# Two layers of graph attention: sending the rows of neighbour maxima of the one-head attentions by way of DRAM

## The chip, the cores and the metric

The kernel runs on one core of a Trainium2 chip. The metric is device time in microseconds (us), from the first to the last instruction of the program on that core. TensorE (PE), VectorE (DVE), ScalarE (ACT), GpSimd (POOL) and SyncE (SP, which here only issues transfers) each run their own queue of instructions in order, and wait for each other by semaphores.

## The reference

There are 32 graphs of 512 nodes with 512 features each, and an adjacency matrix for each graph. All values are float32. Two layers follow each other, each with a layer norm and a ReLU ahead and a residual added behind:

```python
# layer 0: one head
h = jnp.maximum(_layernorm(x), 0.0)
scores = leaky_relu(s_src[:, :, None] + s_dst[:, None, :] + attn_b[0], 0.2)
scores = jnp.where(adj + eye == 0, -inf, scores)
x = x + einsum('bij,bjh->bih', softmax(scores, axis=-1), h)
# layer 1: a four-head attention, then a one-head attention
h = jnp.maximum(_layernorm(x), 0.0)
h = elu(gat_layer(h, mask, W1, att_src1, att_dst1, b1, concat=True))   # 4 heads of 256
x = x + gat_layer(h, mask, W2, att_src2, att_dst2, b2, concat=False)   # 1 head of 512
```

Inside `gat_layer` the nodes are projected (`xl = x @ W`), each node gets two scores from `xl`, the score of an edge is `leaky_relu(asrc + adst)`, edges that are not there are masked, a softmax runs over the neighbours, and the weighted rows of `xl` are summed. So each graph has six attentions: one of layer 0, four heads, and one more of the second layer. In the kernel the first and the last of these are the one-head attentions, called layer 0 and layer 2; the heads are called layer 1.

## The kernel before

A graph's 512 nodes are T = 4 tiles of 128 partitions. Every attention goes through `edge_weights` (L582), which fills a buffer `E` of 128 x 4 x 512 with the unnormalised softmax weights, and through aggregation on PE (L627), which multiplies these weights with the values. The two projections are products of seven half-size blocks (`products`, L822).

`edge_weights` needs three rows that are the same in all 128 partitions: `a_row` (one score of all 512 nodes), `c_row` (the other score) and `m_row` (the greatest score over the neighbours of each node, which keeps the exponent in range). The work for one attention is:

- Row `a` is put in a PSUM bank. DVE takes, for each tile, the maximum of row and mask over the neighbours (L591), and two small operations (L596, L598) make of it the column `m` (128 x 4: the maximum of each node).
- Column `m` is made into a row: for each tile, PE transposes the column broadcast over 128 columns (`spread`, which calls `pe_transpose`, L487). Its result stays in the bank `m_bank`.
- For each of the four tiles: ACT computes the leaky ReLU of row `c` plus a column (L609), DVE subtracts the row `m` (L612), POOL adds the mask (L614), ACT takes the exponent (L617).

Rows `a` and `c` go another way for all but two attentions (layer 0 of graph 0 and layer 2 of graph 31, which use `spread`): `in_lines` (L547) transposes the columns of all scores at once (L553), an engine evicts the result, one transfer writes it to DRAM as lines of 512 values (L559), and `row_of` (L564) reads a line back with the same values for every partition (L569). For row `a`, ACT copies the row into a bank (`in_bank`, L576).

The places: `E` has 3, `E_one` (the weights of a one-head attention) has 2, `a_row` and `c_row` have one each, and the eight PSUM banks are six `acc`, one `a_bank` and one `m_bank`. The accumulators of projections and aggregations, and the transposes that precede an eviction, use `acc`.

The order of the work is written by a planner (`Plan`) while the program is built. Each operation is entered with an engine or a choice of engines, a modelled cost, and the buffers that it reads and writes. `draft` runs a list schedule over all operations: an engine takes the most urgent operation whose inputs are done and whose new buffers find a vacant place; buffers whose kind is listed as `in_turn` take their places in the order of entry. `latest` works out from a draft by when each operation must be done; six drafts are made, and the one that ends first is emitted. `AHEAD` makes an operation more urgent in the first draft. The modelled time from issue to landing is 3.0 us for lines and 4.5 us for a row.

Operations are entered graph by graph: projection of layer 1, aggregation of layer 2 of the graph before, the four heads, aggregation of layer 0 of the next graph (`layer0_out`), the scores of layer 0 of the graph after that (`layer0_scores`), projection of layer 2 and its edge weights (`layer2_project`). The planner moves them from there.

Of the kernel before, what the change touches and what calls it, by code (L numbers as in the profile page):

```python
# [15 lines left out]
P = 128  # L16
# [244 lines left out]
def kernel(  # L261
# [24 lines left out]
    nc = tc.nc  # L286
    B, N, D = x.shape
    H, F = att_src1.shape
    HF = H * F
    T = N // P  # L290
# [10 lines left out]
    psum = ctx.enter_context(tc.tile_pool(name="psum", bufs=1, space=PSUM))  # L301
# [11 lines left out]
    def places(kind, n, shape, dtype=F32, pool=big):  # L313
        return [pool.tile(shape, dtype, tag=f"{kind}{k}", name=f"{kind}{k}") for k in range(n)]
# [14 lines left out]
        "v": places("v", 2, [P, T, F]),  # L329
        "e": places("e", 1, [P, T // 2, F]),  # L330
        "col": places("col", 12, [P, T]),
        "ac": places("ac", 5, [P, 4, T]),
        "a_row": places("a_row", 1, [P, N]),
        "c_row": places("c_row", 1, [P, N]),
        "r": places("r", 8, [P, 1]),
        "st": places("st", 1, [P, T, nc.vector.BN_STATS_DIM]),
        "mv": places("mv", 1, [P, T, nc.vector.BN_AGGR_DIM]),
        "acc": places("acc", 6, [P, 512], pool=psum),
        "a_bank": places("a_bank", 1, [P, 512], pool=psum),
        "m_bank": places("m_bank", 1, [P, 512], pool=psum),  # L340
    }
    junk = big.tile([P, 512], BF16, name="junk")
    spill = ctx.enter_context(tc.tile_pool(name="spill", bufs=1, space=bass.MemoryType.DRAM))
    slots["spill"] = places("spill", 2, [N, D], pool=spill)
    slots["lines"] = places("lines", 8, [4, N], pool=spill)
    plan = Plan(slots, ("x", "spill", "m0", "m0T", "m1", "m1T", "h", "hT", "pair", "xl2", "E", "E_one", "v", "a_row", "c_row", "a_bank"))
    op = plan.op


    ident = const.tile([P, P], F32, name="ident")  # L350
# [30 lines left out]


    AHEAD, LATER = 400, 300


    QUARTER = (("11", "T1"), ("21", "22"))
# [142 lines left out]

        op(("ACT", "DVE"), (on_act(n, bias is not None), on_dve(n)), (by_act, by_dve), src, dst)  # L530

    def spread(kind, part, col_of, ahead):

        row = Buffer(kind)
        for t in range(T):
            pe_transpose(
                ahead, row, lambda t=t: row.at[:, node_block(t)], part, lambda t=t: col_of(t).to_broadcast([P, P]), ident, t
            )
        return row
# [4 lines left out]
        evict(values, ac(0), cols_of, place_of, 4 * T)  # L544
        return ac

    def in_lines(ac, part, n):  # L547

        pt, flat_, lines = Buffer("acc"), Buffer("e"), Buffer("lines")
        m = n * T  # L550
        op(
            "PE", on_pe(P, transpose=True),
            lambda: nc.tensor.transpose(pt.at[:m, :P], ac.at[:, :n, :].rearrange("p n t -> p (n t)"), ident),  # L553
            part + flat_("place"), pt(0), AHEAD,
        )
        evict(pt(0), flat_(0), lambda: pt.at[:m, :P], lambda: flat_.at[:m, 0, :P], P)
        op(
            "SP", by_dma(4 * m * P, 3000.0),
            lambda: nc.sync.dma_start(lines.at[:n].rearrange("n (t p) -> (n t) p", p=P), flat_.at[:m, 0, :P]),  # L559
            flat_(0), lines(0), AHEAD,  # L560
        )
        return lines

    def row_of(kind, lines, k):  # L564

        row = Buffer(kind)
        op(
            "SP", by_dma(4 * P * N, 4500.0),
            lambda: nc.sync.dma_start(  # L569
                row.at, bass.AP(tensor=lines.at.tensor, offset=lines.at.offset + k * N, ap=[[0, P], [1, N]])  # L570
            ),
            lines(0), row(*ROW), AHEAD,
        )
        return row

    def in_bank(kind, row):  # L576

        bank = Buffer(kind)
        op("ACT", on_act(N), lambda: nc.scalar.copy(bank.at, row.at), row(*ROW), bank(*ROW), AHEAD)
        return bank  # L580

    def edge_weights(kind, scores, ac, lines, k, mask_max, mask):  # L582


        a_of = lambda t: ac.at[:, k, t : t + 1]
        a_row = spread("a_bank", scores, a_of, AHEAD) if lines is None else in_bank("a_bank", row_of("a_row", lines, k))
        amax, z, m = Buffer("col"), Buffer("col"), Buffer("col")
        for t in range(T):
            op(
                "DVE", on_dve(N + 60),  # L590
                lambda t=t: nc.vector.tensor_tensor_reduce(  # L591
                    junk, mask_max.at[:, t, :], a_row.at, 1.0, LOWEST, ALU.add, ALU.max, accum_out=amax.at[:, t : t + 1]
                ),
                a_row(*ROW) + mask_max(*ROW), amax(t),
            )
        op("DVE", on_dve(T), lambda: nc.vector.tensor_add(z.at, ac.at[:, k + 1, :], amax.at), scores + amax(*ROW), z(0))  # L596
        op(
            "DVE", on_dve(T), lambda: nc.vector.scalar_tensor_tensor(m.at, z.at, SLOPE, z.at, op0=ALU.mult, op1=ALU.max),  # L598
            z(0), m(0),
        )  # L600

        E = Buffer(kind)
        m_row = spread("m_bank", m(0) + E("place"), lambda t: m.at[:, t : t + 1], AHEAD)
        c_of = lambda t: ac.at[:, k + 1, t : t + 1]
        c_row = spread("acc", scores + E("place"), c_of, AHEAD) if lines is None else row_of("c_row", lines, k + 1)
        for t in range(T):
            op(
                "ACT", on_act(N, 1),
                lambda t=t: nc.scalar.activation(E.at[:, t, :], c_row.at, AF.Prelu, bias=a_of(t), scale=1.0, alpha=SLOPE),  # L609
                c_row(*ROW) + scores, E(t),  # L610
            )
            op("DVE", on_dve(N), lambda t=t: nc.vector.tensor_sub(E.at[:, t, :], E.at[:, t, :], m_row.at), m_row(*ROW) + E(t), E(t))  # L612
            op(
                "POOL", on_pool(N, True), lambda t=t: nc.gpsimd.tensor_add(E.at[:, t, :], E.at[:, t, :], mask.at[:, t, :]),  # L614
                E(t) + mask(*ROW), E(t), lock=True,
            )
            op("ACT", on_act(N), lambda t=t: nc.scalar.activation(E.at[:, t, :], E.at[:, t, :], AF.Exp), E(t), E(t))  # L617
        return E
# [32 lines left out]
    X, S, M, L0, HT, L1, AC, H1T, L2 = {}, {}, {}, {}, {}, {}, {}, {}, {}  # L651
# [56 lines left out]
    def layer0_scores(b):  # L708
        rstd, nmr = layernorm(X[b])
        h0, ac = Buffer("h"), Buffer("ac")  # L710
        for t in range(T):
            relu_normed(h0, X[b], t, rstd, nmr)
            for i, w in ((1, ws_r), (0, wd_r)):
                op(
                    "DVE", on_dve(D), lambda t=t, w=w, i=i: dot(h0.at[:, t, :D], w, ac.at[:, i, t : t + 1]),
                    h0(t) + W["w0"](0, 1), ac((i, t)), lock=True,
                )
        c = ac(*((1, t) for t in ROW))
        op(
            "DVE", on_dve(T), lambda: nc.vector.tensor_scalar(ac.at[:, 1, :], ac.at[:, 1, :], b0_r, None, op0=ALU.add),  # L720
            c + W["w0"](2), c,
        )
        m0, m0T = masks0(b)
        scores = c + ac(*((0, t) for t in ROW))

        L0[b] = (h0, edge_weights("E_one", scores, ac, in_lines(ac, scores, 2) if b else None, 0, m0, m0T))

    def layer0_out(b):
        h0, E = L0.pop(b)
# [141 lines left out]
    def layer1_scores(b, h):  # L871
        xl, j = L1[b][h // 2], h % 2
        m1, m1T = M[b]
        if j == 0:
            ac = gather(
                xl(*((i, t) for t in range(T) for i in range(2))),
                lambda: xl_of(xl)[:, :, :, :2].rearrange("p t j i -> p j i t"), lambda: ac.at.rearrange("p (j i) t -> p j i t", j=2),
            )
            AC[b] = (ac, in_lines(ac, ac(0), 4))
        ac, lines = AC[b]  # L880
        return edge_weights("E", ac(0), ac, lines, 2 * j, m1T, m1)

    def layer1_head(b, h, E):

# [41 lines left out]
    def layer2_project(b):  # L926
        h1T = H1T.pop(b)
        L1.pop(b)
        m1, m1T = M.pop(b)

        xl = Buffer("xl2" if b < B - 1 else "pair")
        if b == B - 1:
            op("POOL", (110.0, 120.0), lambda: nc.gpsimd.memset(xl2_of(xl)[:, :, 2 + D :], 1.0), (), xl(2))

        def dst(i, j, r, c):
            t = i * (T // 2) + r
            return xl((j, t)), lambda: xl2_of(xl)[:, t, j * W2 : (j + 1) * W2]

        products(
            lambda i, j: h1T_of(h1T[j])[:, :, i * HN : (i + 1) * HN],  # L940
            lambda i, j, g: h1T[j](*((2 * g + k, i) for k in range(2))),
            PER, weights_of("w2", KINDS_2), W2, range(1), lambda w, k, c: w2_s[w][:, k, :], dst, [xl],
        )
        ac = gather(
            xl(*((0, t) for t in range(T))), lambda: xl2_of(xl)[:, :, :2].rearrange("p t i -> p i t"), lambda: ac.at[:, :2, :]
        )
        L2[b] = (edge_weights("E_one", ac(0), ac, in_lines(ac, ac(0), 2) if b < B - 1 else None, 0, m1T, m1), xl)

    def xl2_of(buf):
        return buf.at if buf.kind == "xl2" else buf.at[:, : T * (2 + D + 1)].rearrange("p (t f) -> p t f", t=T)  # L950
# [82 lines left out]
```

## Time and profile before

| | before |
|---|---|
| time | 3692.82 us, median of 3 runs (3692.64 to 3694.01) |
| profiled span | 3692.5 us |
| PE, weight loads (PEld), DVE, ACT, POOL busy | 98%, 85%, 78%, 48%, 43% |
| mean granted TensorE clock | 0.996 |
| matmuls on `m_bank` (L487) | 768, 117.1 us busy |
| line transposes (L553) | 126 (64 of 16 columns, 62 of 8) |
| copies of row `a` to its bank (L579) | 190, 582 ns each |
| rows read from DRAM | 190 of `a`, 190 of `c`, 256 KB each |

Busy times of PE overlap, since matmuls are pipelined: the time that an instruction costs is read from the distance between starts. In the timeline, a line merges instructions of one kind that follow each other; brackets at its end give the engine's idle time before it, and what ended it.

### The profile page before, as it was taken

To read this page: it belongs to the slowest core of one execution; us is meant where nothing else is said; L and a number is where in the kernel's file an instruction comes from. 1 tells how busy PE (TensorE), PEld (TensorE's weight loads), DVE (VectorE), ACT (ScalarE), POOL (GpSimd) and SP (SyncE) were. 2 spreads that over 40 slices of the span, in tenths; PEclk is the share of its full clock that TensorE was granted. 3 is DMA by queue.
4 is the path that set the end of the run, shared out by engine and by line. 5 is a ranking of instruction groups with operands and counts; after the bars stand their busy time and mean duration, and the time that the engine had idled before them with its cause. 6 is when DMAs were issued, how large, how long until landed. Compare 5 with 4: busy or idle time off the path is not lost.

```text
span 3692.5 us, 51317 instructions
## 1 busy us (share of the span) xinstructions
PE 3625.2 (98%) x17806; PEld 3131.3 (85%) x17806; DVE 2878.2 (78%) x7478; ACT 1760.2 (48%) x3227; POOL 1592.1 (43%) x1353
## 2 busy tenths in 40 slices
PE   5899999999999999999999999999999999999998
PEld 4788888888888888888888888888888888888887
DVE  7988778877788877788877878777887778787755
ACT  2455444554454554445544445544455544455433
POOL 3534444534444444445344444444444444444332
PEclk9999999999999999999999999999999999999999
DMA  6244322334323333223333233442233422334310
GB/s 162 52 92 103 87 73 82 81 92 104 72 74 90 75 103 91 70 83 80 91 103 72 76 88 75 103 98 68 81 82 85 103 72 78 86 75 103 90 51 32
DMA packets 304342, 312.17 MB, mean 85 GB/s; under 512 B 150496, under 2 KB 188880, under 8 KB 304080
## 3 DMA queue, kind: packets, MB, share of 16 engines
q1 hardware_dynamic: 270288, 275.32, 26.2%
q0 software_dynamic: 33792, 33.56, 6.5%
q8 instruction: 140, 2.29, 0.3%
q14 instruction: 122, 1.00, 0.1%
HBM read 240.91 MB, written 67.89 MB: 84 GB/s over the span
## 4 chain that ended last, share of the span: by engine, by line
PE 94%; DVE 3%; DMA 1%; POOL 0%; issue 0%; ACT 0%; DVEq 0%; ACTq 0%
PE acc L627 46%; PE acc L822 41%; PE acc L487 4%; PE m_bank L487 2%; DVE junk L591 1%; DVE junk L378 0%; PE acc L553 0%; DVE E L612 0%; DMA m<-in_adj_dram 0%; DVE v L905 0%; POOL E_one L614 0%; DVE E_one L612 0%; DMA x<-in_x_dram 0%; DVE v L893 0%; DMA out_dram<-x 0%
## 5 line engine op out<-in xcount | busy, mean ns | idle before, releaser
L614 POOL TENSOR_TENSOR E<-E,m 128x512 f32<-128x512 f32 x512 | 620.2, 1240 | 803.3 <-DVE E L612 798.3
L627 PE MATMUL acc<-pair,E 128*128 128x257 f32 x4096 | 961.6, 381 | 1.4 <-ACT E L617 1.2
L627 PEld LDWEIGHTS acc<-pair,E 128*128 128x128 f32 x4096 | 743.0, 190 | 114.5 <-ACT E L617 14.4
L822 PE MATMUL acc<-w_T,E 128*128 128x257 f32 (+1 forms) x2048 | 521.5, 381 | 1.0 <-ACT pair L522 0.6
L627 PE MATMUL acc<-h,E_one 128*128 128x256 f32 (+1 forms) x2048 | 478.2, 382 | 6.3 <-ACT E_one L617 6.3
L617 ACT ACTIVATE E<-E 128x512 f32<-128x512 f32 x512 | 312.0, 624 | 315.4 <-POOL E L614 315.4
L627 PE MATMUL acc<-xl,E_one 128*128 128x257 f32 x1984 | 448.2, 379 | 0.0
L591 DVE CUSTOM_DVE_ANT_0 junk<-m1T,a_bank 128x512 bf16<-128x512 bf16 x640 | 436.0, 681 | 15.4 <-PE a_bank L487 1.7
L627 PEld LDWEIGHTS acc<-h,E_one 128*128 128x128 f32 x2048 | 383.8, 191 | 59.4 <-ACT E_one L617 7.6
L822 PEld LDWEIGHTS acc<-w_T,E 128*128 128x128 f32 x2048 | 379.6, 190 | 55.4 <-ACT pair L522 0.8
L627 PEld LDWEIGHTS acc<-xl,E_one 128*128 128x128 f32 x1984 | 371.4, 190 | 53.7
L612 DVE TENSOR_TENSOR E<-E,m_bank 128x512 f32<-128x512 f32 x512 | 326.5, 679 | 24.7 <-PE m_bank L487 24.7
L609 ACT ACTIVATE E<-c_row,ac 128x512 f32<-128x512 f32 x512 | 335.6, 708 | 1.9 <-DMA c_row<-lines 1.9
L520 ACT COPY pair<-acc 128x258 f32<-128x258 f32 (+1 forms) x375 | 138.2, 369 | 412.1 <-PE acc L822 410.3
L520 ACT COPY xl<-acc 128x257 f32<-128x257 f32 x219 | 81.7, 373 | 455.8 <-PE acc L822 455.8
L902 ACT ACTIVATE e<-v,minus_one 128x512 f32<-128x512 f32 x256 | 184.3, 720 | 236.4 <-DVE r L639 111.1
L645 DVE SCALAR_TENSOR_TENSOR x<-acc,r,x 128x256 f32<-128x256 f32 x512 | 240.6, 478 | 47.8 <-PE acc L627 43.6
L663 POOL DMA_DIRECT2D m<-in_adj_dram x64 | 51.4, 804 | 521.1 <-DVE col L591 476.8
L835 DVE TENSOR_TENSOR pair<-acc,pair 128x258 f32<-128x258 f32 (+1 forms) x390 | 164.5, 424 | 137.8 <-PE acc L822 127.7
L822 PE MATMUL acc<-w,hT 128*128 128x258 f32 x1024 | 268.4, 382 | 0.0
L822 PE MATMUL acc<-w,pair 128*128 128x257 f32 x1024 | 259.3, 380 | 0.0
L614 POOL TENSOR_TENSOR E_one<-E_one,m 128x512 f32<-128x512 f32 x128 | 145.0, 1165 | 263.2 <-DVE E_one L612 263.2
(108 smaller groups left out, 6117.7 us busy)
## 6 DMA issues: line engine op xcount, KB each, us to landing
a_row<-lines SPq DMA_DIRECT2D x190, 256.0 KB, 3.4
c_row<-lines SPq DMA_DIRECT2D x190, 256.0 KB, 3.5
x<-in_x_dram SPq DMA_DIRECT2D x32, 1024.0 KB
m<-in_adj_dram POOLq DMA_DIRECT2D x64, 512.0 KB, 7.0
spill<-x SPq DMA_DIRECT2D x32, 1024.0 KB, 4.3
x<-spill SPq DMA_DIRECT2D x32, 1024.0 KB
out_dram<-x SPq DMA_DIRECT2D x30, 1024.0 KB, 5.0
m0T<-m SPq DMA_TRANSPOSE x128, 4.2
```

The source lines that it names most:

```text
L487: op("PE", on_pe(P, transpose=True), lambda: nc.tensor.transpose(dst_of(), src_of(), identity), src, dst(part), ahead)
L520: nc.scalar.copy(dst_of(), src_of())
L591: lambda t=t: nc.vector.tensor_tensor_reduce(junk, mask_max.at[:, t, :], a_row.at, 1.0, LOWEST, ALU.add, ALU.max, accum_out=amax.at[:, t : ...
L609: lambda t=t: nc.scalar.activation(E.at[:, t, :], c_row.at, AF.Prelu, bias=a_of(t), scale=1.0, alpha=SLOPE),
L612: op("DVE", on_dve(N), lambda t=t: nc.vector.tensor_sub(E.at[:, t, :], E.at[:, t, :], m_row.at), m_row(*ROW) + E(t), E(t))
L614: "POOL", on_pool(N, True), lambda t=t: nc.gpsimd.tensor_add(E.at[:, t, :], E.at[:, t, :], mask.at[:, t, :]),
L617: op("ACT", on_act(N), lambda t=t: nc.scalar.activation(E.at[:, t, :], E.at[:, t, :], AF.Exp), E(t), E(t))
L627: lambda s=s: nc.tensor.matmul(acc.at[:, :n], E.at[:, s, node_block(t)], of(s), start=(s == 0), stop=(s == T - 1)),
L645: lambda acc=acc, r=r, f=f, t=t: nc.vector.scalar_tensor_tensor(X.at[:, t, f], acc.at[:, :HD], r.at, X.at[:, t, f], op0=ALU.mult, op1=ALU. ...
L822: lambda k=k: nc.tensor.matmul(acc.at[:, :width], at[a]()[:, k, node_block(r)], weight_of(w, k, c), start=(first and k == 0), stop=(k == n ...
L835: op("DVE", on_dve(width), lambda: nc.vector.tensor_add(place(), acc.at[:, :width], place()), acc(0) + token, token)
L902: op("ACT", on_act(2 * F, 1), lambda e=e, ts=ts: nc.scalar.activation(e.at, v.at[:, ts, :], AF.Exp, bias=minus_one), parts, e(0))
```

## The change

Row `m` of most one-head attentions takes the way that rows `a` and `c` already take: the column `m` is transposed into four lines by one transpose, evicted, written to DRAM, read back as a row in all partitions, and copied into a bank. This is for fewer transposes on PE. Layer 0 of graph 0, layer 2 of graph 31 and all heads of layer 1 keep `spread`; the names `NEAR0`, `NEAR2` and `FAR` choose. So that three kinds of rows can pass, the banks become eight places of one kind `acc`, and the two row places become two of one kind `row`; neither kind is taken in turn. The small buffer `ac` loses one of its five places.

```diff
-        "ac": places("ac", 5, [P, 4, T]),
-        "a_row": places("a_row", 1, [P, N]),
-        "c_row": places("c_row", 1, [P, N]),
+        "ac": places("ac", 4, [P, 4, T]),
+        "row": places("row", 2, [P, N]),
...
-        "acc": places("acc", 6, [P, 512], pool=psum),
-        "a_bank": places("a_bank", 1, [P, 512], pool=psum),
-        "m_bank": places("m_bank", 1, [P, 512], pool=psum),
+        "acc": places("acc", 8, [P, 512], pool=psum),
...
-    plan = Plan(slots, ("x", "spill", "m0", "m0T", "m1", "m1T", "h", "hT", "pair", "xl2", "E", "E_one", "v", "a_row", "c_row", "a_bank"))
+    plan = Plan(slots, ("x", "spill", "m0", "m0T", "m1", "m1T", "h", "hT", "pair", "xl2", "E", "E_one", "v"))
...
+    NEAR0, NEAR2, FAR = False, False, ()
...
-    def edge_weights(kind, scores, ac, lines, k, mask_max, mask):
+    def edge_weights(kind, scores, ac, lines, k, mask_max, mask, near):
...
-        a_row = spread("a_bank", scores, a_of, AHEAD) if lines is None else in_bank("a_bank", row_of("a_row", lines, k))
+        a_row = spread(scores, a_of, AHEAD) if lines is None else in_bank(row_of(lines, k))
...
-        m_row = spread("m_bank", m(0) + E("place"), lambda t: m.at[:, t : t + 1], AHEAD)
+        m_row = (
+            spread(m(0) + E("place"), lambda t: m.at[:, t : t + 1], AHEAD) if near
+            else in_bank(row_of(in_lines(lambda: m.at, m(0), 1), 0))
+        )
...
-        L0[b] = (h0, edge_weights("E_one", scores, ac, in_lines(ac, scores, 2) if b else None, 0, m0, m0T))
+        L0[b] = (h0, edge_weights("E_one", scores, ac, in_lines(first(ac, 2), scores, 2) if b else None, 0, m0, m0T, not b or NEAR0))
...
-        return edge_weights("E", ac(0), ac, lines, 2 * j, m1T, m1)
+        return edge_weights("E", ac(0), ac, lines, 2 * j, m1T, m1, h not in FAR)
...
-        L2[b] = (edge_weights("E_one", ac(0), ac, in_lines(ac, ac(0), 2) if b < B - 1 else None, 0, m1T, m1), xl)
+        L2[b] = (edge_weights("E_one", ac(0), ac, in_lines(first(ac, 2), ac(0), 2) if b < B - 1 else None, 0, m1T, m1, b == B - 1 or NEAR2), xl)
```

The new row of `m` does not ask for a place of `E` before it is made (`E("place")` stands only in the `spread` branch).

More of the change, by code (lines that the diff above doesn't have):

```diff
@@ L530, in evict, with spread @@
         op(("ACT", "DVE"), (on_act(n, bias is not None), on_dve(n)), (by_act, by_dve), src, dst)
-    def spread(kind, part, col_of, ahead):
-        row = Buffer(kind)
+    def spread(part, col_of, ahead):
+        row = Buffer("acc")
         for t in range(T):
@@ L545, in gather, with first, in_lines @@
         return ac
-    def in_lines(ac, part, n):
+    def first(ac, n):
+        return lambda: ac.at[:, :n, :].rearrange("p n t -> p (n t)")
+    def in_lines(cols_of, part, n):
         pt, flat_, lines = Buffer("acc"), Buffer("e"), Buffer("lines")
@@ L552, in in_lines @@
             "PE", on_pe(P, transpose=True),
-            lambda: nc.tensor.transpose(pt.at[:m, :P], ac.at[:, :n, :].rearrange("p n t -> p (n t)"), ident),
+            lambda: nc.tensor.transpose(pt.at[:m, :P], cols_of(), ident),
             part + flat_("place"), pt(0), AHEAD,
@@ L562, in in_lines, with row_of @@
         return lines
-    def row_of(kind, lines, k):
-        row = Buffer(kind)
+    def row_of(lines, k):
+        row = Buffer("row")
         op(
@@ L574, in row_of, with in_bank @@
         return row
-    def in_bank(kind, row):
-        bank = Buffer(kind)
+    def in_bank(row):
+        bank = Buffer("acc")
         op("ACT", on_act(N), lambda: nc.scalar.copy(bank.at, row.at), row(*ROW), bank(*ROW), AHEAD)
         return bank
-    def edge_weights(kind, scores, ac, lines, k, mask_max, mask):
+    def edge_weights(kind, scores, ac, lines, k, mask_max, mask, near):
         a_of = lambda t: ac.at[:, k, t : t + 1]
-        a_row = spread("a_bank", scores, a_of, AHEAD) if lines is None else in_bank("a_bank", row_of("a_row", lines, k))
+        a_row = spread(scores, a_of, AHEAD) if lines is None else in_bank(row_of(lines, k))
         amax, z, m = Buffer("col"), Buffer("col"), Buffer("col")
@@ L602, in edge_weights @@
         E = Buffer(kind)
-        m_row = spread("m_bank", m(0) + E("place"), lambda t: m.at[:, t : t + 1], AHEAD)
+        m_row = (
+            spread(m(0) + E("place"), lambda t: m.at[:, t : t + 1], AHEAD) if near
+            else in_bank(row_of(in_lines(lambda: m.at, m(0), 1), 0))
+        )
         c_of = lambda t: ac.at[:, k + 1, t : t + 1]
-        c_row = spread("acc", scores + E("place"), c_of, AHEAD) if lines is None else row_of("c_row", lines, k + 1)
+        c_row = spread(scores + E("place"), c_of, AHEAD) if lines is None else row_of(lines, k + 1)
         for t in range(T):
@@ L878, in layer1_scores @@
             )
-            AC[b] = (ac, in_lines(ac, ac(0), 4))
+            AC[b] = (ac, in_lines(first(ac, 4), ac(0), 4))
         ac, lines = AC[b]
-        return edge_weights("E", ac(0), ac, lines, 2 * j, m1T, m1)
+        return edge_weights("E", ac(0), ac, lines, 2 * j, m1T, m1, h not in FAR)
     def layer1_head(b, h, E):
```

## The prediction

> **What bounds the kernel now.** I read the busy times first, then the chain that ended last, then the busy time by stretch, then the timeline of single engines inside one period.
>
> ```profile
> PE 3625.2 (98%) x17806; PEld 3131.3 (85%) x17806; DVE 2878.2 (78%) x7478; ACT 1760.2 (48%) x3227; POOL 1592.1 (43%) x1353
> ...
> PE 94%; DVE 3%; DMA 1%; POOL 0%; issue 0%; ACT 0%; DVEq 0%; ACTq 0%
> PE acc L627 46%; PE acc L822 41%; PE acc L487 4%; PE m_bank L487 2%; DVE junk L591 1%; DVE junk L378 0%; PE acc L553 0%; DVE E L612 0%; DMA m<-in_adj_dram 0%; DVE v L905 0%; POOL E_one L614 0%; DVE E_one L612 0%; DMA x<-in_x_dram 0%; DVE v L893 0%; DMA out_dram<-x 0%
> ```
>
> TensorE (PE) carries 94% of the chain; `m_bank`, the maxima rows that the change touches, has 2% of it. The busy times by stretch say where PE is not full:
>
> ```profile
> 394.99:507.60 112.61, 112.61 (x557) 97.49 (x557) 88.59 (x231) 55.01 (x102) 49.40 (x43) 1.00 0.34 85
> 507.60:620.22 112.62, 112.62 (x558) 97.50 (x557) 88.56 (x230) 54.59 (x102) 49.41 (x43) 1.00 0.33 85
> 180.00:3560.00 3380.00, 3377.76 (x16670) 2922.95 (x16669) 2653.12 (x6878) 1641.89 (x3011) 1478.82 (x1257) 1.00 0.33 85
> ```
>
> Columns: stretch, length, then PE, PEld, DVE, ACT, POOL busy (instructions), granted clock, DMA share, GB/s. One graph takes 112.61 us, of which PE is busy 112.61; VectorE (DVE) has 24 us free, ScalarE (ACT) 57. A busy PE need not be at its peak, so I recount from starts. In the PE timeline of a middle period, a block of eight matmuls starts at 1420.18 and the next block at 1421.92: 0.2175 us each. A graph has 480 such instructions (15,360 / 32) and 76 transposes (`v` 32, `m_bank` 24, `h` 16, lines 4). Transposes in the same timeline (start, duration, engine, line, operation):
>
> ```profile
> 1429.32 0.27 PE L553 MATMUL acc<-ident,ac 128*8 128x128 f32 x1
> 1429.42 0.60 PE L822 MATMUL acc<-w,hT 128*128 128x258 f32 x2
> ...
> 1433.34 0.60 PE L487 MATMUL m_bank<-ident,col 128*128 128x128 f32 x4
> 1433.78 0.60 PE L822 MATMUL acc<-w_T,E 128*128 128x258 f32 x2
> ```
>
> The four transposes of a row take 0.44 us from start to the next start, 0.11 each (the 275 ns in the group table is latency, overlapped). The 128x8 transpose into lines also costs 0.10 to 0.11. 480 x 0.2175 + 76 x 0.11 = 112.8, the period. So PE issues back to back; every transpose removed is worth 0.11 us, provided nothing new makes it wait.
>
> **What the Trainium skill says.** Perfetto Trace Analysis, "Identifying the Most-Contended Engine", warns that matmul busy share is a poor sign of the limit and asks for weight-load busy share too: here 85%, and the recount agrees that PE is the bound. TensorE: Matmul & The Clock Gate, "Part 4: PE-mode transpose", gives about 275 ns for a transpose in a kernel's context; the trace agrees as a duration (273 to 275 ns), but its pitch is 0.11 us, which I use. DMA: Bandwidth & Descriptors, "Anatomy of one DMA", puts about 2 us of fixed time on a transfer, mostly the write receipt; here lines land in 2.5 us (8 KB) and rows in 3.5 us. That is why the new route is long in latency though small in work. PSUM — Partial Sum Buffer, "Specifications (TRN2)", counts 8 banks: the kernel uses all of them before and after; only their division changes.
>
> **Part 1: transposes removed and added.** 62 one-head attentions change route: layer 0 of graphs 1 to 31 and layer 2 of graphs 0 to 30 (`not b or NEAR0`, `b == B - 1 or NEAR2`). `FAR` is empty, so all 128 layer-1 heads keep the spread. Removed: 62 x 4 = 248 transposes. Added: 62 line transposes of 128x4, not seen in before; bounds 0 and 0.11 us; the 128x8 and 128x16 forms both show 0.11, which I take. Net 186 x 0.11 = 20.4 us at the bound engine, 0.66 us a graph. Full value: 3692.8 - 20.4 = 3672.4.
>
> **Part 2: work added elsewhere.** On ACT 62 evictions of a line (254 ns in the 8x128 row) and 62 copies row to bank (582 ns): 52 us in all, 1.7 a graph, beside 57 free. DVE does the same reductions and subtractions from a bank as before. SP issues 124 more transfers at about 0.33 us; DMA moves 62 x 256 KB = 16 MB more, 5% of 312 MB, at a DMA share of 0.33. All of it lies beside the saturated PE: nothing.
>
> **Part 3: the new wait.** From a finished `m` to its bank it took a transpose and its queueing. Now: transpose 0.3, eviction 0.25, lines 2.5, row 3.5, copy 0.6, some signals and SP issue: about 7.8 us. Who waits: the four subtractions (L612) on DVE, then POOL's mask addition, ACT's exponent, and the aggregation on PE.
>
> Layer 0: in the middle period its reductions run at 1429.4, its weights are done at 1439.9, and its first aggregation is at 1482.7. 43 us of slack against at most 7.8: hidden. Layer 2:
>
> ```profile
> 1443.23 0.15 DVE L598 SCALAR_TENSOR_TENSOR col<-col 128x4 f32<-128x4 f32 x1
> ...
> 1445.84 1.28 DVE L612 TENSOR_TENSOR E_one<-E_one,m_bank 128x512 f32<-128x512 f32 x2
> ```
> ```profile
> 1451.15 0.63 ACT L617 ACTIVATE E_one<-E_one 128x512 f32<-128x512 f32 x1 [0.49 <-POOL E_one L614]
> ```
> ```profile
> 1451.73 1.03 PE L627 MATMUL acc<-xl,E_one 128*128 128x257 f32 x4
> ```
>
> Here `m` is ready at 1443.4, the last exponent ends at 1451.8, and PE begins to aggregate at 1451.73: no slack. With the bank ready at 1443.4 + 7.8 = 1451.2 instead of 1445.6 these weights come 5.6 us late, up to 3 less if the planner brings the reductions (1439.6) nearer to the row's landing (about 1435). PE need not idle: the 64 aggregations of layer 0 (13.9 us) have their weights by 1440, or 1447 with their own delay, and stand later only as filler between the heads (1482 to 1513). The order is rebuilt from modelled times (lines 3.0, row 4.5, above the measured ones), so I expect 2 to 6 us of filler to move ahead. The heads then need less filler, since the same delay gives their weights more lead. Steady cost taken: 0; ends 0 and 31 x 5.6 = 174.
>
> **Part 4: the two ends.** The first stretch has PE idle:
>
> ```profile
> 95.74 1.11 PE L487 MATMUL m_bank<-ident,col 128*128 128x128 f32 x4 [5.14 <-DVE col L598]
> 99.60 13.93 PE L627 MATMUL acc<-h,E_one 128*128 128x257 f32 x54 [2.54 <-ACT E_one L617]
> ```
>
> This is layer 0 of graph 1; PE already waits for its `m`. The route adds up to 6.6 us (103.5 against 96.9). But DVE is busy 95% from 80 to 100 and about 90% to 180, and PE loses another 6 us in small waits from 116 to 165, some of which the moved aggregation can fill. I take +3, ends 0 and 6.6. At the tail there is no following layer 0 as filler: layer 2 of graph 30 starts its aggregation at 3590.91, 1.7 us after its weights, with projection work to 3592.6. A delay of 4 to 6.5 less that slack costs +2, ends 0 and 5. Layer 2 of graph 31 is unchanged.
>
> **Part 5: places.** Six `acc` banks plus one each for `a` and `m` become eight of one kind; row places are shared and no longer taken in turn. A bank held by a row (about 4 us for `a`, 3 for `m`, six times a period) is 0.4 of a bank on average, so accumulators mostly gain. PE waits for no bank in the middle, so I credit nothing; the price could be rows holding banks early. Sum: 3692.8 - 20.4 + 3 + 2 = 3677.4.
>
> **Rivals.** *All hidden*: planner covers the ends as well, 3672.4. For it: the busy DVE in the first stretch; against: the two waits just shown. Chance 0.19. *Layer 2 waits in each graph* (slower): zero slack at 1451.7, and each engine runs its queue in order, so a subtraction placed too early stalls accumulator evictions on DVE and then PE. If all but 1.5 us of the delay is filled: 3677.4 + 31 x 1.5 = 3723.9; at 0.9 us it is 3705.3, which I name as its time. Against: 14 us of ready filler. Chance 0.14. *Banks or rows starve*: early rows hold two or more banks in the projection, or SP waits with mask transposes behind it (1.25 us each to issue). A loss of 0.4 us a graph gives 3689.8. Against: reductions free a bank in 3 us. Chance 0.07.
>
> **How the numbers follow.** My forecast, 3677.4, has chance 0.60, with its ends from Part 4 at 3672.4 to 3684. The range 3668 to 3698 takes in all hidden with a few us of luck in the first stretch, and starvation; it leaves out most of the slower case and a little at each side, below 2 in 10. Faster by 0.2% means below 3685.4: 0.60 and 0.19 less a little, 0.77. Same 0.09 (starvation and the upper edge), slower 0.14.
>
> **What would show it.** Right: 520 `m` transposes instead of 768, line transposes 188 instead of 126, a period near 111.95 with PE full, aggregations of layer 0 before those of layer 2 in each period, and PE idle a few us more before 180. Wrong: PE idle inside a period before layer 2's aggregation or behind an eviction, or a period above 112.6.

## The result, and the profile after

The changed kernel takes 3677.09 us (median of 4 runs, 3675.71 to 3678.40) against 3692.73 of the kernel before, run beside it: a ratio of 0.9958, 95% interval 0.994 to 0.9975. It is 15.6 us faster.

The page of the changed kernel has these lines in place of the first ones shown of before (L631, L826 and L485 are now aggregation, projection and transposes; rows of maxima lie in `acc` like all else):

```profile
PE 3598.6 (98%) x17620; PEld 3118.9 (85%) x17620; DVE 2953.4 (80%) x7487; ACT 1873.2 (51%) x3426; POOL 1456.5 (40%) x1269
...
PE 95%; DVE 2%; ACT 0%; POOL 0%; issue 0%; DVEq 0%
PE acc L631 47%; PE acc L826 42%; PE acc L485 6%; PE acc L554 1%; DVE junk L592 1%; DVE E L616 0%; DVE x L649 0%; DVE E_one L616 0%; DVE st L491 0%; ACT E_one L621 0%; DVE v L897 0%; DVE w L457 0%; POOL E L618 0%; POOL E_one L618 0%; DVE junk L375 0%
```

PE has 186 instructions fewer (17806 to 17620), the count of the prediction, and still carries the chain. In its table of groups, the transposes of columns fall from 768 to 520, and 62 of a new form appear:

```profile
L485 PE MATMUL acc<-ident,col 128*128 128x128 f32 x520 | 79.5, 276 | 20.1 <-DVE col L599 20.1
...
L554 PE MATMUL acc<-ident,col 128*4 128x128 f32 x62 | 17.0, 274 | 5.4 <-DVE col L599 5.4
```

Busy times by stretch, with the columns of the prediction; the second line is the first stretch, in which PE was busy 125.45 us before:

```profile
507.85:619.67 111.82, 111.82 (x551) 97.15 (x551) 91.10 (x231) 58.56 (x108) 44.71 (x40) 1.00 0.35 90
...
0.00:180.00 180.00, 118.93 (x541) 100.05 (x542) 150.76 (x433) 67.43 (x120) 79.63 (x70) 0.91 0.42 112
```

From the issues of the transfer `spill<-x`, one for each graph, the time divides into three:

| | before | after | difference |
|---|---|---|---|
| start to the 5th issue | 509.08 | 510.52 | +1.4 |
| the 24 periods to the 29th issue | 112.613 each | 111.835 each | -18.7 |
| 29th issue to the end | 480.7 | 481.2 | +0.4 |

So the middle gave 0.78 us a graph where the count of transposes gives 0.66, and the two ends gave back a part. How much each end gave back is not to be read from the times alone, since the two kernels have not issued the same work up to the fifth `spill`. Busy times up to it, all instructions and then the transposes, before:

```profile
0.00:509.08 509.08, 452.29 (x2169) 385.65 (x2170) 417.86 (x1101) 234.55 (x427) 227.02 (x192) 0.98 0.38 93
0.00:509.08 509.08, 56.14 (x327) 42.19 (x327) 8.28 (x25) 0.50 (x2) 0.98 0.38 93
```

and after (in the lines of transposes the engines are PE, PEld, DVE, POOL):

```profile
0.00:510.52 510.52, 449.16 (x2164) 385.98 (x2165) 422.23 (x1113) 240.00 (x436) 214.09 (x186) 0.97 0.37 97
0.00:510.52 510.52, 51.44 (x306) 38.70 (x306) 5.88 (x25) 0.50 (x2) 0.97 0.37 97
```

PE had 1842 matmul instructions and 327 transposes behind it before, and has 1858 and 306 after. Thus 16 matmul instructions (3.5 us) have moved from the tail to the front, and 21 transposes (2.3 us) fell away in front; of the other 165, 144 fell away in the middle and 21 in the tail. Against its work the front is therefore 1.4 - 3.5 + 2.3 = 0.2 us slower, and the tail 0.4 + 3.5 + 2.3 = 6.2 us.

Before 180 us PE is idle 61.1 us instead of 54.6. The timeline of PE in that stretch of the changed kernel:

```profile
93.37 0.37 PE L554 MATMUL acc<-ident,col 128*4 128x128 f32 x1 [5.41 <-DVE col L599]
105.33 1.11 PE L485 MATMUL acc<-ident,col 128*128 128x128 f32 x4 [11.59 <-DVE col L599]
109.19 9.34 PE L631 MATMUL acc<-pair,E 128*128 128x257 f32 x32 [2.74 <-ACT E L621]
120.71 7.20 PE L631 MATMUL acc<-h,E_one 128*128 128x257 f32 x32 [1.75 <-ACT E_one L621]
```

Layer 0 of graph 1 (`h,E_one`), which PE began at 99.60 before, now begins at 120.7, behind head 0 of graph 0, and PE stands 11.6 us with nothing to do until that head's maxima are there.

A middle period, PE's timeline of the changed kernel:

```profile
1428.21 0.60 PE L826 MATMUL acc<-w_T,E 128*128 128x258 f32 x2
1428.64 0.27 PE L554 MATMUL acc<-ident,col 128*4 128x128 f32 x1
1428.75 1.04 PE L826 MATMUL acc<-w,E 128*128 128x258 f32 x4
...
1439.31 0.27 PE L554 MATMUL acc<-ident,col 128*4 128x128 f32 x1
...
1442.90 1.03 PE L631 MATMUL acc<-h,E_one 128*128 128x257 f32 x4
...
1455.57 3.63 PE L631 MATMUL acc<-pair,E 128*128 128x257 f32 x16
1459.04 0.60 PE L631 MATMUL acc<-xl,E_one 128*128 128x257 f32 x2
```

The 128x4 transpose costs 0.11 us from start to start. After the projection PE aggregates layer 0 (1442.9), then the first of a head (1455.6), and only then layer 2 (1459.0), which came first before. No line between has brackets: PE never stands.

### The profile page after: what moved, and what is told of

It is laid out like the page before. It is cut to its first block, busy times and chain, and to the rows that moved or that the text cites. A ratio compares the mean times of both kernels' runs of the same rounds, so it can differ in the third digit from the quotient of the medians.

```text
span 3675.7 us, 51476 instructions
## 1 busy us (share of the span) xinstructions
PE 3598.6 (98%) x17620; PEld 3118.9 (85%) x17620; DVE 2953.4 (80%) x7487; ACT 1873.2 (51%) x3426; POOL 1456.5 (40%) x1269
## 4 chain that ended last, share of the span: by engine, by line
PE 95%; DVE 2%; ACT 0%; POOL 0%; issue 0%; DVEq 0%
PE acc L631 47%; PE acc L826 42%; PE acc L485 6%; PE acc L554 1%; DVE junk L592 1%; DVE E L616 0%; DVE x L649 0%; DVE E_one L616 0%; DVE st L491 0%; ACT E_one L621 0%; DVE v L897 0%; DVE w L457 0%; POOL E L618 0%; POOL E_one L618 0%; DVE junk L375 0%
## 5 line engine op out<-in xcount | busy, mean ns | idle before, releaser
L631 PE MATMUL acc<-pair,E 128*128 128x257 f32 x4096 | 950.2, 381 | 5.5 <-ACT E L621 5.5
L618 POOL TENSOR_TENSOR E<-E,m 128x512 f32<-128x512 f32 x512 | 596.6, 1189 | 769.6 <-DVE E L616 527.5
L631 PEld LDWEIGHTS acc<-pair,E 128*128 128x128 f32 x4096 | 760.0, 190 | 110.1 <-ACT E L621 7.1
L826 PE MATMUL acc<-w_T,E 128*128 128x257 f32 (+1 forms) x2048 | 517.9, 380 | 0.0
L631 PE MATMUL acc<-h,E_one 128*128 128x256 f32 (+1 forms) x2048 | 479.7, 381 | 4.8 <-ACT E_one L621 4.8
L592 DVE CUSTOM_DVE_ANT_0 junk<-m1T,acc 128x512 bf16<-128x512 bf16 x640 | 436.2, 682 | 29.1 <-ACT acc L580 16.5
L631 PE MATMUL acc<-xl,E_one 128*128 128x257 f32 x1984 | 459.6, 379 | 0.0
L826 PEld LDWEIGHTS acc<-w_T,E 128*128 128x128 f32 x2048 | 383.4, 190 | 61.5 <-DVE E L807 0.2
L631 PEld LDWEIGHTS acc<-h,E_one 128*128 128x128 f32 x2048 | 381.8, 190 | 61.3 <-ACT E_one L621 5.8
L631 PEld LDWEIGHTS acc<-xl,E_one 128*128 128x128 f32 x1984 | 370.5, 189 | 50.8 <-ACT E_one L621 0.7
L613 ACT ACTIVATE E<-row,ac 128x512 f32<-128x512 f32 x512 | 343.7, 708 | 80.9 <-PE acc L631 78.1
L518 ACT COPY pair<-acc 128x258 f32<-128x258 f32 (+1 forms) x486 | 181.4, 374 | 380.2 <-PE acc L826 376.1
L906 ACT ACTIVATE e<-v,minus_one 128x512 f32<-128x512 f32 x256 | 184.8, 722 | 317.8 <-DVE v L897 221.8
L616 DVE TENSOR_TENSOR E<-E,acc 128x512 f32<-128x512 f32 x512 | 324.5, 674 | 3.4 <-PE acc L485 3.2
L618 POOL TENSOR_TENSOR E_one<-E_one,m0T 128x512 f32<-128x512 f32 x128 | 144.8, 1155 | 335.9 <-DVE E_one L616 335.8
L826 PE MATMUL acc<-w,hT 128*128 128x258 f32 x1024 | 268.1, 381 | 0.0
L826 PE MATMUL acc<-w,E 128*128 128x257 f32 (+1 forms) x1024 | 267.6, 381 | 0.0
L909 DVE SCALAR_TENSOR_TENSOR v<-e,v 128x512 f32<-128x512 f32 x256 | 225.6, 881 | 44.0 <-ACT e L906 42.3
L667 POOL DMA_DIRECT2D m<-in_adj_dram x64 | 51.5, 805 | 502.2 <-DVE col L592 465.9
```

Source lines behind the costliest of these rows:

```text
L518: nc.scalar.copy(dst_of(), src_of())
L592: lambda t=t: nc.vector.tensor_tensor_reduce(junk, mask_max.at[:, t, :], a_row.at, 1.0, LOWEST, ALU.add, ALU.max, accum_out=amax.at[:, t : ...
L631: lambda s=s: nc.tensor.matmul(acc.at[:, :n], E.at[:, s, node_block(t)], of(s), start=(s == 0), stop=(s == T - 1)),
L826: lambda k=k: nc.tensor.matmul(acc.at[:, :width], at[a]()[:, k, node_block(r)], weight_of(w, k, c), start=(first and k == 0), stop=(k == n ...
L906: op("ACT", on_act(2 * F, 1), lambda e=e, ts=ts: nc.scalar.activation(e.at, v.at[:, ts, :], AF.Exp, bias=minus_one), parts, e(0))
L909: lambda e=e, ts=ts: nc.vector.scalar_tensor_tensor(v.at[:, ts, :], e.at, 1.0, v.at[:, ts, :], op0=ALU.min, op1=ALU.max),
```

## The experiments

Three periods help to read them. The changed kernel has 70 transposes a graph in 111.835 us, and its matmuls show no wait there; I take that as issue time. With 0.109 us for each further transpose, 73 make 112.16 and 76 make 112.49. What a period takes above this I count as waiting of PE. (Such waits of up to 0.8 us lie mostly ahead of weight loads; since the matmuls on record overlap, PE's busy time hides them.) By this the kernel before waited 0.12 us a graph. What the weight loads waited for from 400 to 3400 us (total, times, longest), in the kernel before and in the changed one:

```profile
PEld acc L627 <- ACT E L617: 9.9, 55, 0.2
```
```profile
PEld acc L554 <- DVE col L599: 4.9, 27, 0.2
```

The second of these costs the period nothing: in the timeline above, the two matmul instructions ahead of the line transpose at 1428.64 take 0.43 us from start to start, as two take elsewhere.

**Banks and row places alone.**

```diff
-    NEAR0, NEAR2, FAR = False, False, ()
+    NEAR0, NEAR2, FAR = True, True, ()
```

> All rows of maxima stay on the spread (768 transposes); only the eight shared banks and the two shared row places of the change are kept. Theory 1 (the gain is the issue time of the removed transposes on PE): the steady period stays at 112.6 us (112.5 to 112.7) and the time within 4 us of the kernel before, 3689 to 3697. Theory 2 (the gain comes from the freed and shared banks): the period falls to about 112.0 and the time to about 3680.

Measured: 3683.73 us, ratio 0.9976 (0.9966 to 0.9986); period 112.583. Both theories missed half of it. The period stays, as theory 1 said, but the time falls by 9 us: the fifth `spill` is issued at 501.28 instead of 509.08, a gain of 7.8 us ahead of the middle. Busy times by stretch of the kernel before, then of this run:

```profile
0.00:180.00 180.00, 125.45 (x560) 104.09 (x561) 153.63 (x421) 67.90 (x121) 81.10 (x69) 0.94 0.41 103
```
```profile
0.00:180.00 180.00, 128.51 (x580) 106.22 (x581) 156.74 (x439) 69.18 (x123) 81.55 (x69) 0.94 0.42 107
```

PE and DVE are each busy 3.1 us more before 180 us than in the kernel before, and PE another 2.1 us more from 180 to 500 (319.9 instead of 317.8). Up to the fifth `spill` PE has issued the same counts in both, 1842 and 327, so the 7.8 us are a gain in full. Whether the banks, the rows, or only the order that the planner wrote with them brings it was not taken apart.

**The route alone, with banks divided as before.**

```diff
-        "acc": places("acc", 8, [P, 512], pool=psum),
+        "acc": places("acc", 6, [P, 512], pool=psum),
+        "a_bank": places("a_bank", 1, [P, 512], pool=psum),
+        "m_bank": places("m_bank", 1, [P, 512], pool=psum),
```

> The rows of maxima of the one-head attentions go by way of DRAM, but the banks are divided as before: six for accumulators, one for the row a, one for the row m. Theory 1: period 111.8 to 112.0 us, time 3675 to 3684. Theory 2 (shared banks are needed for the gain): the period stays at 112.5 or more, PE waits for banks, and the time is 3690 or more.

Measured: 3692.40 us, ratio 1.0001 (0.9993 to 1.001); periods alternate 112.14 and 112.91, mean 112.53. Theory 1 fails: PE issues 186 transposes fewer and gains nothing, because it waits 0.69 us a graph. The longest of the waits of its weight loads, as above:

```profile
PEld acc L487 <- DVE v L911: 18.3, 42, 0.7
```

By the trace it is not for a bank, as theory 2 would have it, but mostly for DVE's last operation on a head's result ahead of its transposes. The two row places stay shared here, and no bank is taken in turn, so this is not the division of before in every point. And it is one order of the planner's: whether the route gains with divided banks in another order was not run.

**Layer 0 alone, layer 2 alone.**

```diff
-    NEAR0, NEAR2, FAR = False, False, ()
+    NEAR0, NEAR2, FAR = False, True, ()     # layer 0 alone
+    NEAR0, NEAR2, FAR = True, False, ()     # layer 2 alone
```

> Only layer 0 (graphs 1 to 31) sends its maxima by way of DRAM; layer 2 spreads. Theory 1: the period falls by half of the counted 0.66, to 112.28 us (112.15 if the small waits of the heads on their exponents vanish too); PE idle before 180 us is about 61 us as after the change, since the loss in the first stretch comes from layer 0 of graph 1; time about 3689. Theory 3 (the 0.12 us a period above the count comes from layer 2's later place in the order): period 112.28 and no less here.

> Only layer 2 (graphs 0 to 30) sends its maxima by way of DRAM; layer 0 spreads. Theory 1: period 112.28 us, PE idle before 180 us about 55 us as before the change, idle in the tail about 10 us as after it; time about 3685. Theory 3 (the 0.12 us a period above the count comes from layer 2's later place in the order): period 112.15, and layer 0 is aggregated ahead of layer 2 in every graph.

Measured, one run each: 3690.75 and 3695.66 us; periods 112.638 and 112.704 (the latter alternating 112.5 and 112.9). Both periods should have been 112.16 to 112.28. PE waits 0.48 and 0.54 us a graph. Weight loads of layer 0 alone, then of layer 2 alone:

```profile
PEld acc L631 <- ACT E L621: 15.1, 52, 0.3
```
```profile
PEld acc L485 <- DVE v L909: 14.5, 28, 0.8
PEld acc L631 <- ACT E L621: 7.4, 27, 0.4
```

What is waited for are a head's exponents and its results, though no head was changed. Theory 3 says nothing here, since neither period fell. Theory 1 holds for the first stretch: idle before 180 us is 60.6 with layer 0 alone and 51.8 with layer 2 alone, so the idle time there is layer 0's.

**Layer 0 of graph 1 spread again; and layer 2 of graph 30 as well.**

```diff
-        ... not b or NEAR0))
+        ... b < 2 or NEAR0))
-        ... b == B - 1 or NEAR2), xl)
+        ... b >= B - 2 or NEAR2), xl)     # second run only
```

> As the changed kernel, but layer 0 of graph 1 spreads its maxima too (four transposes more, one line transpose fewer). Theory 1 (the shared banks gain in the first stretch, and the DRAM route of this one attention gives it back): PE idle before 180 us falls from 61 to about 52 us as with the banks alone, the period stays at 111.84, time about 3669 (3666 to 3672). Rival (the loss of the first stretch is a matter of the plan as a whole): idle stays at 58 to 61, time 3675 to 3679.

> As the run before in this list, and layer 2 of graph 30 spreads its maxima as well. Theory 1: the tail's idle (3.6 us ahead of a head's maxima and 2.75 ahead of its weights at 3572 to 3580) falls by about 3 us; period 111.84; time about 3666. Rival: the tail's wait is that of head 0 of the last graph, not of layer 2, so that the tail stays as it is: no faster than the run before.

Measured: 3695.13 us (ratio 1.0006, 0.9997 to 1.0015) and 3690.70 us (0.9994, 0.9985 to 1.0002). The ends do as theory 1 said: idle before 180 us is 51.5 and 52.1, and after 3400 us it falls from 15.2 in the first run to 10.8 in the second, which is 4.4 us faster. But the times forecast, 3669 and 3666, were missed by 26 and 25 us, since in both the period is 112.684: PE waits 0.85 us in graphs whose operations were not touched. So I looked for the cause in the order that the planner wrote around the edit.

**The same operations in another order.** The planner makes six drafts and keeps the one that its own model ends first. The next kernels take a fixed draft.

```diff
-        for _ in range(self.DRAFTS):
+        for k in range(4):
...
-            if best is None or draft.end < best.end:
+            if k == 3:
```

> The kernel that spreads the maxima of layer 0 of graph 1 and layer 2 of graph 30, in the order of its fourth draft instead of its third (model: 3658.5 and 3655.4). Theory 4: the waits of 0.85 us a period seen in its third draft are that order's, and differ here by more than 0.2 us a period; with a wait near 0 the time is about 3666. Rival (the waits come with these two spreads): period 112.6 to 112.7 again, time about 3691.

> The changed kernel, operation for operation, in the order of the planner's fourth draft instead of its fifth (the planner's own model puts the two 1.5 us apart: 3663.3 and 3661.7). Theory 4 (what a period costs above its issue time depends on the order that the planner happens to emit, since its costs miss small times of the chip): the issue time stays at 111.84 a period, but PE's waits differ, a period of 112.0 to 112.8, time 3680 to 3695. Rival (the change itself leaves PE no waits): period 111.84 again, time within 4 us of 3677.

Measured: with the two spreads 3674.65 us (0.9949, 0.9935 to 0.9964), period 111.854; the changed kernel in its fourth draft 3679.96 us (0.9964, 0.9951 to 0.9977), period 111.841. The first is theory 4 at its plainest: identical operations, 3690.70 in one order and 3674.65 in the other. One middle period of each, by stretch (third draft, then fourth), and the waits of weight loads:

```profile
1400.00:1512.66 112.66, 112.38 (x552) 96.92 (x551) 90.80 (x228) 59.14 (x110) 46.71 (x40) 1.00 0.34 90
```
```profile
PEld acc L485 <- ACT h L508: 23.9, 52, 0.6
PEld acc L826 <- DVE pair L839: 5.7, 27, 0.2
PEld acc L554 <- DVE col L599: 4.8, 27, 0.2
PEld acc L631 <- DVE col L592: 4.6, 27, 0.4
```
```profile
1400.00:1511.83 111.83, 111.83 (x552) 97.15 (x551) 91.14 (x231) 58.57 (x107) 44.69 (x39) 1.00 0.35 90
```
```profile
PEld acc L554 <- DVE col L599: 4.9, 27, 0.2
PEld acc L826 <- DVE E L807: 0.4, 1, 0.4
```

In the third draft the transposes of `h` wait for ACT's normalised rows in each graph; in the fourth that wait is gone. The one that stays, on the line transposes, costs nothing in the period. For the changed kernel the rival was right: its fourth draft keeps the period, and the 3 us more lie ahead of the middle (fifth `spill` at 513.7 instead of 510.5). So the order decides, but this kernel had two good orders. The losses of the route alone and of the half changes were each seen in one order, and don't show that the shared banks or both routes are needed. With both ends spread in a good order the median is the lowest of all, 2.4 us below the changed kernel; the two intervals overlap, so it is not shown to be faster than it. What it gains lies at the tail (476.3 us behind the 29th issue instead of 481.2); in front nothing comes of the spread of layer 0 of graph 1 here: idle before 180 us is 54.7, but the fifth `spill` comes at 512.2, not before the 510.5 of the changed kernel.

**The modelled costs.** From start to start the traces show 0.73 us for a reduction over a row and for a dot product on DVE where the planner's costs say 0.67 and 0.60, and 0.61 for the leaky ReLU on ACT where they say 0.57. (The 0.73 is that of the dot products with `wd_r`. Those with `ws_r` have a median duration of 1.4 us in the changed kernel against 0.69, and the costs stay too low for them; why they are longer is open.)

```diff
-    one = n / 1.2 + (95.0, 140.0, 280.0)[per_partition]
+    one = n / 1.2 + (110.0, 190.0, 280.0)[per_partition]
...
-                "DVE", on_dve(N + 60),
+                "DVE", on_dve(N + 122),
```

(and 122 more elements for the dot products, at four places)

> The changed kernel with five modelled costs set to what the traces show between starts (reductions over a row and dot products on DVE 0.73 us instead of 0.67 and 0.60, ACT with a bias column 0.045 us more, without one 0.012 us more); the operations are the same. The planner's model now ends at 3681. Theory 4: order and chip agree better, measured time 3681 to 3695 less far above the model than the 15 to 36 us of the other runs, with the period above 111.84. Rival (the costs don't matter): the time stays within 4 us of 3677.

> The same two spreads with the five costs corrected; the planner's model ends at 3678. Theory 4: time within 12 us of the model, 3678 to 3690. Rival (as before the correction): about 3691 with PE waiting 0.85 us a period.

Measured: 3687.62 us (0.9984, 0.9977 to 0.9992), period 111.895; and 3682.19 us (0.997, 0.9959 to 0.9982), period 111.892. Both hold theory 4's ranges. For the kernel with both ends spread the wait of 0.85 is now 0.06: for the period, correcting costs is as good as choosing another draft. But the gain is lost at the ends; in the second the fifth `spill` comes at 514.2, against 505.9 uncorrected, so this is no better kernel. The profile of the first is of its fastest run, so 5 us of its median lie in no trace. The times of the first spread over 8 us (3682.4 to 3690.6), with a granted clock of 0.996 in the fastest run and 0.993 in the slowest.

**A longer wait.** The line of maxima is copied once more from DRAM to DRAM.

```diff
-            else in_bank(row_of(in_lines(lambda: m.at, m(0), 1), 0))
+            else in_bank(row_of(again(in_lines(lambda: m.at, m(0), 1)), 0))
```

> As the changed kernel, but the line of maxima is copied once more from DRAM to DRAM before it is read as a row, which makes the added wait longer by one transfer, some 2 to 3 us. Theory 1 (the wait is hidden in the middle by layer 0's aggregations): the period stays within 0.15 us of 111.84. Rival (the wait has no reserve left): the period grows by 0.5 us or more.

Measured, one run: 3749.65 us, periods alternating 112.5 to 114.1 and 115.2, mean 114.34. The rival holds: in the order that the planner wrote for it there is no reserve for one more transfer. PE (not only its loads) waits for layer 0's weights, which had become the filler and now come late themselves:

```profile
PE acc L639 <- ACT E_one L629: 28.8, 13, 2.2
```

**All attentions by way of DRAM.**

```diff
-    NEAR0, NEAR2, FAR = False, False, ()
+    NEAR0, NEAR2, FAR = False, False, (0, 1, 2, 3)
```

> As the changed kernel, but the heads of layer 1 also send their maxima by way of DRAM: 12 transposes a graph fewer on PE, issue time 110.52 us a period. Theory 1 (a removed transpose is worth its issue time only where other aggregations fill the added wait): the heads have no such reserve, PE waits for their exponents, and the period is above 111.84. Rival (every removed transpose is worth 0.11 us): period 110.5, time about 3635.

Measured, one run: 3927.19 us, 119.5 us a graph, with 12 transposes fewer in each. Theory 1 holds:

```profile
PE acc L631 <- ACT E L621: 123.6, 25, 7.4
```

PE waits up to 7.4 us for a head's exponents. For the heads the DRAM route costs far more than four transposes, in the one order that was run; the granted clock was lower too, 0.968 on average.

## Why the prediction was right, point by point

It forecast 3677.4; 3677.09 came out. Its terms fare differently, and errors that cancel make the match: that it holds to 0.3 us is luck.

- *Part 1, transposes.* Right: 520 and 188 counted, 0.11 us for the 128x4 form. 186 x 0.109 = 20.3 us.
- *Part 2, work elsewhere.* Right: it lies beside PE. In the middle DVE is busy 91.1 of 111.8 us and ACT 58.6.
- *Part 3, the new wait.* The outcome is right (steady cost 0, layer 0 ahead of layer 2), the size is not. From `m` to bank it took 10.1 us in layer 0 (1428.5 to 1438.6) and 16.7 in layer 2 (1434.3 to 1451.0), not 7.8, since PE's queue has layer 2's line transpose 5 us after `m` (1439.31), and SP issues the row at 1447.0, behind two mask transposes. Layer 2's last weights end 18.1 us after the last product's start at 1443.8; before, they ended 0.8 ahead of it. The filler was 52 of layer 0's 64 matmuls and 16 of a head, 68 x 0.2175 = 14.8 us, not 2 to 6.
- *The steady cost of 0 was not safe.* The longer wait and the half changes show how near it is: with the route in whole or in half, and other orders, the graph costs 0.5 to 0.85 us in waits, more than or about as much as the saving. The rival "layer 2 waits in each graph" named that size, 0.9 us, rightly, but not where it waits: the runs showed heads' exponents and results, and the transposes of `h`. Against these runs my chance of 0.14 for it looks low.
- *A term that I left out.* The small waits of the kernel before, 0.12 us a graph, went away too: 24 x 0.12 = 2.9 us gained in the middle.
- *Part 4, the ends.* +3 and +2 were forecast. Against its work the front is 0.2 us slower and the tail 6.2. The tail's term was right in kind and too small: PE stands 3.6 us ahead of the maxima of the last graph's head 0 and 2.75 ahead of its weights (3572 to 3580), and with layer 2 of graph 30 spread again the tail was 4.4 us shorter. The 6.2 lie outside the range of 0 to 5. The sum 6.4 stands for 5.
- *Part 5, places.* This step failed: "I credit nothing". With the shared places alone the first stretch was 7.8 us shorter, in one order of the planner's. Against the run with the banks alone, the fifth `spill` of the changed kernel then comes 9.2 us later (501.28 to 510.52). With the 16 matmul instructions moved forward and the 21 transposes that fell away, the step to the DRAM route costs 9.2 - 3.5 + 2.3 = 8.0 us there in these two orders, not 3: "some of which the moved aggregation can fill" didn't happen, since the planner put head 0 ahead and layer 0 of graph 1 came 21 us later. A gain of 7.8 us that was not forecast and a loss 5 us greater than forecast met inside the term for the first stretch.

Together: -20.3 - 2.9 + 0.2 + 6.2 = -16.8, as between the two profiled spans.

## What to carry to other kernels

Where one engine issues back to back, an instruction removed is worth its distance between starts, not its duration; but only if no new wait eats it, and a saving of 0.66 us in 112 is smaller than the waits that two orders of the same work differ by. So judge such a change by several orders (another draft, another edit of the same kind) and by issue time and waits apart, not by one time. A detour through DRAM of 8 us on paper took 10 to 17 in a busy schedule: give it to work that other work can stand in for, and price both ends of the program apart. And before comparing the times of two orders up to some mark, count the work that each has issued by then.

## What was not expected of the hardware

Idle time of PE can cost twice. After two gaps of 14.3 us together between 93.7 and 109.2 us, 32 matmuls took from 109.19 to the next start at 118.36, 0.29 us each instead of 0.2175; the granted clock was 0.76 in that stretch. At the end of the kernel before, behind two gaps of 2.7 us, the last 64 matmuls took 16.7 us at a mean granted clock of 0.84; behind one gap of 2.75 us in the changed kernel they took 14.1 at 1.00. And the mean clock moves though nothing in the program does: from 0.993 to 0.996 over the runs of one kernel (that with corrected costs), with 8 us between the times.
